# Expert numbers 21 to a register load, table sums three blocks at once, and a written order for SP in a mixture-of-experts stage

## The chip, the cores and the metric

The kernel runs on one core of a Trainium2 chip. A core has five engines that run side by side, each with its own instruction stream: TensorE (PE in the profile; PEld is its weight load), VectorE (DVE), ScalarE (ACT), GpSimd (POOL) and SyncE (SP, which mostly starts DMAs). They wait for each other through semaphores. The metric is device time in microseconds (us) of one launch; smaller is better. For several launches the median is given.

## The reference

An image of 2 x 256 channels x 56 x 56 goes through a convolution-like layer (group means and a ReLU), then through a transformer layer over N = 3136 tokens of 256 numbers for each of the two images: causal attention with four heads, and then a top-2 mixture of eight experts. The last part is what the change touches:

```python
t = t + _L1_attn_ref(_ln_t(t), L1_attn_W_attn, L1_attn_W_proj)
t = t + _L1_ffn_ref(_ln_t(t), L1_ffn_gate_w, L1_ffn_gate_b, ...)
...
probs = jax.nn.softmax(xf @ gate_w + gate_b, axis=-1)
top2_vals, top2_idx = jax.lax.top_k(probs, 2)
cw = jnp.zeros((N, Ee)).at[jnp.arange(N)[:, None], top2_idx].add(top2_vals)
for each expert e:
    out += cw[:, e] * (gelu(xf @ w1[e] + b1[e]) @ w2[e] + b2[e])
```

The loop over the experts is a scan in the reference; it is shortened here. Width 256, hidden width 512, all in 32-bit floats.

## The kernel before, in words

The kernel computes only the two experts that each token picks, so 2 x 2 x 3136 rows in all. It sorts these rows by expert into slots of a table in DRAM, in blocks of 128 slots that belong to one expert each: NBLK = 105 blocks.

**Dispatch.** `dispatch(b)` runs once for each of the two images, b = 0 and 1: softmax of the gate, top two, a rank for every picked row (matmuls into `rank` and `total`), the slot of each row, the expert of each block (`eblks[b]`), the biases of the blocks (matmuls into `bp`). Then POOL scatters the rows, two indirect DMAs from each of NCH = 25 tiles `xr`, to the table `xds[b]` (L1108). The tiles of image 1 come from a pool `sx` of 10 buffers. The first FULL0 = 42 blocks hold rows of image 0 alone. The blocks up to MIXED = 57 may hold rows of both images, and these are in two tables: a block's input there is the sum of its rows of both.

**Experts.** `experts` (L1124) is the stage from about 895 to 1352 us. Its loop runs n from -1 to 107 and does in iteration n, in written order:

- `fetch(g)`: starts the DMA of a group of GB = 3 blocks from the table to a tile `xb` (three buffers), six blocks ahead; for groups 14 to 18 also that of the other table to `xo` (one buffer).
- `load(g)`: two blocks ahead; for image 1 the tokens to which results go (`to`), and a register load (L1162) of the three experts of the group, one on PE and one on DVE, because both address weights by the expert's number.
- `hidden(n)`: eight matmuls into `ht` (L1202) and four Gelu on ACT to `g` (L1211).
- `inputs(n + 1)`: for blocks 42 to 56 adds the block's `xo` rows to its `xb` rows on DVE (L1176); two transposes on PE into `tp` (L1179) and a copy on ACT to `xT` (L1183).
- `weights(n + 2)`: DVE copies the expert's first weights to `w` (L1190), at an address taken from a register.
- `outputs(n - 3)`: four matmuls into `yp` (L1220) with the expert's second weights in `w2s`, also addressed by a register; DVE adds the bias to give `ys` (L1228); blocks below 57 are stored by SP to `y_slots`, blocks from 42 on are scattered by POOL to `y_tokens` (L1234).
- `between()`: pulls two pieces of other work (three while image 1's rows are being scattered) from a queue of generators.

**The queue of other work.** `pull` (L1359) takes the first generator that has something to do. `yield True` ends a piece of work, `yield False` says that nothing can be done yet. In the queue are `closing` (the end of attention, then `judge`), `tokens` with the rest of `dispatch(1)`, and from block 57 on `finish(0)`, which gathers image 0's results from `y_slots` and writes them out. `finish(1)` runs after the loop. `judge` (L1343) looks at the largest and the smallest row sum of the softmax and counts, with a matmul into `gdp`, whether all lie within bounds; the number `good` is read by all engines at the end, where the program branches on it.

**Attention's end.** The last block of attention is scaled while the expert stage begins: `sum_rows` (a matmul into `sp` L681, a copy to `line` L686, DMAs), `invert` (reciprocals, DMAs to `inverses` and `rb`), `scale` (L713), then the projection into `pp` (L563).

**What sets the order.** Inside `tc.manual_schedule(engines={PE, DVE, POOL})` these three engines run their instructions in the order in which the program is written. ACT and SP are ordered by a scheduler: SP's DMA starts may stand earlier or later in its stream than they are written. A tile waits for a free buffer of its pool before it is written, and a queue that reaches such a wait holds everything behind it.

Of the kernel before, what the change touches and what calls it, by code (L numbers as in the profile page):

```python
# [16 lines left out]
PE = mybir.EngineType.PE  # L17
DVE = mybir.EngineType.DVE
POOL = mybir.EngineType.Pool

MASKED = -1.0e30
LOWEST = -3.0e38
# [3 lines left out]
def conv_attn_moe_kernel(  # L26
# [71 lines left out]
    MIXED = MOST0 + E  # L98
    NBLK = (2 * B * N + E * (P - 1)) // P
    GB = 3  # L100
    SCALE = 1.0 / HS**0.5
    LEAST, MOST = 1e-25, 1e25
    assert B == 2 and NBLK % GB == 0 and FULL0 % GB == 0 and QB % (2 * P) == 0
    assert E % HEADS == 0 and NCH * XW <= NH * E * H

    def chunk(j):
# [318 lines left out]
    def layer1(nm, general):  # L425

        with ExitStack() as whole:
# [471 lines left out]
            def dispatch(b):  # L899
# [59 lines left out]
                flat = both.rearrange("p t e -> p (t e)")  # L959
                yield from small_piece()  # L960


                rank = bank(f"rank_{b}")
                nc.tensor.matmul(rank[:, : NCH * E], keep01, flat, start=True, stop=True)
# [118 lines left out]
                hot = g1.tile([E, w], F32, tag="hot", name=f"hot_{nm}{b}")  # L1083
                nc.vector.tensor_tensor(hot, eb[:E, :w], row.to_broadcast([E, w]), ALU.is_equal)
                yield from small_piece()
                bp = bank(f"bp_{b}", (P, KH, w))
                for k in range(KH):
                    nc.tensor.matmul(bp[:, k, :], b1s[:, k, :], hot, start=True, stop=True)
# [35 lines left out]
            def experts(w1s, w2s, b2s, ex, es, ps6, between, need, written):  # L1124
# [25 lines left out]
                def load(g, xb, other):  # L1150
                    s, e = g * GB, (g + 1) * GB
                    b = 0 if e <= FULL0 else 1
                    to = None
                    if b:

                        eq = es.tile([P, GB], F32, tag="eq", name=f"eq_{nm}_{g}")
                        nc.vector.tensor_tensor(eq, xb[:, :, C + 1], slot_id[:, s:e], ALU.is_equal)
                        nc.vector.tensor_scalar(eq, eq, -float(N), float(N + OFF), ALU.mult, ALU.add)
                        to = ex.tile([P, GB], U32, tag="to", bufs=4, name=f"to_{nm}_{g}")
                        nc.vector.tensor_tensor(to, eq, xb[:, :, C], ALU.add)  # L1160
                    f = known[b][0]
                    _, eids = nc.values_load_multi_w_load_instructions(  # L1162
                        eblks[b][0:1, s - f : e - f],
                        engines=(PE, DVE),
                        min_val=0,
                        max_val=E - 1,
                        skip_runtime_bounds_check_because="a count of at most E parts, cut to E - 1",
                    )
                    return xb, other, to, eids

                def inputs(n, group):
                    xb, other, to, eids = group
                    g = n % GB
                    rows = xb[g] if n < GB else xb[:, g, :C]
                    if FULL0 <= n < MIXED:
                        nc.vector.tensor_tensor(rows, rows, other[:, g, :C], ALU.add)  # L1176
                    tp = ps6.tile([P, 512], F32, tag="tp", bufs=2, name=f"tp_{nm}_{n}")
                    for c in range(NH):
                        nc.tensor.transpose(  # L1179
                            tp[:, c * P : (c + 1) * P], rows[:, c * P : (c + 1) * P], ident  # L1180
                        )
                    xT = es.tile([P, NH, P], F32, tag="xT", name=f"xT_{nm}_{n}")
                    nc.scalar.copy(xT.rearrange("p c t -> p (c t)"), tp[:, : NH * P])  # L1183
                    return xT, to, eids[g]

                def weights(n, group):

                    w = es.tile([P, NH, H], F32, tag="w", bufs=2, name=f"w_{nm}_{n}")
                    e = group[3][n % GB]
                    nc.vector.tensor_copy(  # L1190
                        w, w1s[:, :, bass.ds(e, 1), :].rearrange("p c e h -> p c (e h)")
                    )
                    return w

                def hidden(n, state, w):
                    xT, to, e = state
                    ht = ps6.tile([P, KH, P], F32, tag="ht", bufs=2, name=f"ht_{nm}_{n}")
                    g = es.tile([P, KH, P], F32, tag="g", bufs=LATE + 2, name=f"g_{nm}_{n}")
                    b = int(n >= FULL0)
                    for k in range(KH):  # L1200
                        for c in range(NH):
                            nc.tensor.matmul(  # L1202
                                ht[:, k, :],
                                w[:, c, k * P : (k + 1) * P],
                                xT[:, c, :],
                                start=(c == 0),
                                stop=(c == NH - 1),
                            )
                    for k in range(KH):
                        i = n - known[b][0]  # L1210
                        nc.scalar.activation(  # L1211
                            g[:, k, :], ht[:, k, :], AF.Gelu, bias=b1bs[b][:, k, i : i + 1]
                        )
                    return g, to, e

                def outputs(n, state):
                    g, to, e = state
                    yp = ps6.tile([P, 512], F32, tag="yp", bufs=2, name=f"yp_{nm}_{n}")
                    for k in range(KH):
                        nc.tensor.matmul(  # L1220
# [26 lines left out]
                    if n == MIXED - 1:  # L1247
                        written()

                fetched, groups, xin, wb, act = [], [], {}, {}, {}  # L1250
                for n in range(-1, NBLK + LATE):
                    while len(fetched) * GB <= min(n + 6, NBLK - 1):
                        fetched.append(fetch(len(fetched)))
                    while len(groups) * GB <= min(n + 2, NBLK - 1):
                        groups.append(load(len(groups), *fetched[len(groups)]))
                    if 0 <= n < NBLK:
                        act[n] = hidden(n, xin.pop(n), wb.pop(n))
                    if n + 1 < NBLK:
                        xin[n + 1] = inputs(n + 1, groups[(n + 1) // GB])
                    for m in (n + 1, n + 2):  # L1260
                        if m < NBLK and m // GB < len(groups) and m not in wb:
                            wb[m] = weights(m, groups[m // GB])
                    if 0 <= n - LATE < NBLK:
                        outputs(n - LATE, act.pop(n - LATE))
                    between()
# [77 lines left out]
            def judge():  # L1343

                tiles = g1.tile([P, 4], F32, tag="judge", name=f"judge_{nm}")
                flat_sums = sums.rearrange("p r f -> p (r f)")
                nc.vector.tensor_reduce(tiles[:, 0:1], flat_sums, AX.X, ALU.max)
                nc.vector.tensor_reduce(tiles[:, 1:2], flat_sums, AX.X, ALU.min)
                nc.vector.tensor_scalar(tiles[:, 2:3], tiles[:, 0:1], MOST, None, ALU.is_le)
                nc.vector.tensor_scalar(tiles[:, 3:4], tiles[:, 1:2], LEAST, None, ALU.is_ge)  # L1350
                nc.vector.tensor_tensor(tiles[:, 2:3], tiles[:, 2:3], tiles[:, 3:4], ALU.mult)
                gdp = bank("gdp")
                nc.tensor.matmul(gdp[:1, :1], tiles[:, 2:3], ones[:, 0:1], start=True, stop=True)
                nc.vector.tensor_copy(good, gdp[:1, :1])
# [51 lines left out]

            att = whole.enter_context(ExitStack())
            end = whole.enter_context(ExitStack())
            px = pool(att, "px", bufs=2)
            aw = pool(att, "aw", bufs=1)  # L1410
            kT = aw.tile([P, NH, N], F32, name=f"kT_{nm}")
# [12 lines left out]
            else:  # L1424
# [18 lines left out]
                    while at[b] + 1 < PARTS * (s + 1) and step(b):  # L1443
                        pass

                att.enter_context(tc.manual_schedule(engines={PE, DVE, POOL}))
                for b in range(B):
                    queue.append(tokens(b, qT, lambda b=b: min(finished[b])))

# [23 lines left out]
            def closing():  # L1473

                if not general:
                    while finished[B - 1][NH - 1] < N:
                        clock[0] += 4
                        due(clock[0])
                        yield True
                        yield True  # L1480
                    while not projected[B - 1]:
                        yield False
                    judge()
                end.close()
                scatter_rows.append(pool(whole, "sx", bufs=10, side="right"))
                yield True

            queue.appendleft(closing())
            with ExitStack() as moe:
# [17 lines left out]
                        pull()  # L1507

                def written():
                    oy = pool(moe, "oy", bufs=2, side="right")  # L1510
                    queue.append(finish(0, oy, 2))

                with tc.manual_schedule(engines={PE, DVE, POOL}):
                    experts(
                        first[0], w2s, b2s, ex, es, ps6,
                        lambda: pull(3 if ranked[1] and not sent[1] else 2), need, written,
                    )
# [74 lines left out]
```

## Time and profile before

| | us |
|---|---|
| median of 4 launches | 1396.59 |
| lowest, highest | 1393.25, 1399.71 |
| the profiled launch, its own time | 1399.56 |
| span of the profiled launch | 1397.5 |
| attention and conv layer before the expert stage | 0 to about 895 |
| expert stage | about 895 to 1353 |
| tail (`finish(1)`) | 1353 to 1397.5 |

The page gives busy time of each engine, a table of the span in 40 slices, and the chain of work that ended last, followed back from the last instruction. A group line reads: line of the kernel, engine, operation, output<-input by the program's names, count, busy time and mean length. TENSOR_LOAD is a load of registers; it is run by an engine's sequencer, which the page writes as PEldq, DVEq. "Idle before" is time in which the engine had nothing to run, with the instruction that ended it; "issue" is a wait that the profile does not explain, and "another core or an unknown queue" a semaphore whose setter is not found.

By stage (columns: us, PE busy, PEld busy, DVE busy, ACT busy, POOL busy with instruction counts, the granted share of PE's full clock, busy share of the DMA engines, GB/s):

```profile
410.00:895.00 485.00, 474.90 (x4536) 209.14 (x4528) 336.45 (x547) 256.82 (x355) 91.66 (x71) 1.00 0.11 34
895.00:1353.00 458.00, 420.37 (x2827) 386.97 (x2828) 189.54 (x477) 162.95 (x547) 173.41 (x170) 0.97 0.38 119
1353.00:1397.50 44.50, 15.52 (x55) 9.12 (x53) 21.54 (x51) 7.30 (x13) 1.92 (x2) 0.54 0.69 219
```

How to read it: in the tail PE is busy 15.52 of 44.5 us and the DMA engines 0.69 of it; in the expert stage PE is busy 420.37 of 458.

### The profile page before, as it was taken

Reading aid. Unit: us, or ns where it says so; the run is one execution under the profiler, and the core shown is the slowest. Engines: PE = TensorE matmul, PEld = TensorE weight load, DVE = VectorE, ACT = ScalarE, POOL = GpSimd, SP = SyncE. Lnnn points to the kernel's source line nnn. Section 1 sums busy time; section 2 is a strip of 40 time slices with the busy share of each in tenths; the row PEclk is TensorE's granted clock in tenths of the full one; section 3 lists DMA queues with packets and bytes.
Section 4 is the critical chain, followed back from the end, with each engine's and each line's share of the span. In section 5 each row is a group of like instructions: output and inputs, shape, how many; then the busy total and the mean of one; then the engine's idle time right before and its main releaser. Section 6 shows DMA issues by size and latency. Waiting matters only on the chain.

```text
span 1397.5 us, 27499 instructions
## 1 busy us (share of the span) xinstructions
PE 1305.7 (93%) x10642; PEld 822.9 (59%) x10642; DVE 780.4 (56%) x1525; ACT 610.4 (44%) x1197; POOL 311.3 (22%) x299
## 2 busy tenths in 40 slices
PE   8998999999999999999999999879889998999973
PEld 7864444444444444444444444469789988999872
DVE  1562555757777455677577887547333333444435
ACT  0244554545565554654445565533223333343322
POOL 1102111010000111110333430000562024555530
PEclk9999999999999999999999999999999999999995
DMA  9992000000000001000011123442433233444427
GB/s 299 382 310 88 23 15 25 28 12 20 16 9 23 8 1 37 16 9 16 31 42 43 54 71 119 132 138 63 139 125 96 91 103 100 129 140 138 127 83 246
DMA packets 107889, 123.89 MB, mean 89 GB/s; under 512 B 18863, under 2 KB 97340, under 8 KB 107624
## 3 DMA queue, kind: packets, MB, share of 16 engines
q1 hardware_dynamic: 89976, 89.67, 20.8%
q0 software_dynamic: 10416, 26.00, 5.6%
q10 hardware_dynamic: 7360, 6.39, 1.4%
q8 instruction: 87, 1.43, 0.5%
q14 instruction: 50, 0.41, 0.1%
HBM read 63.04 MB, written 60.81 MB: 89 GB/s over the span
## 4 chain that ended last, share of the span: by engine, by line
PE 73%; issue 9%; DMA 3%; ACT 2%; another core or an unknown queue 1%; DVE 1%; POOL 1%; DVEq 0%; POOLq 0%; ACTq 0%; SPq 0%
PE yp_f L654 17%; PE sc_f L614 17%; PE ht_f L1202 12%; PE yp_f L1220 12%; PE qk_f L513 5%; PE pp_f L563 3%; PE v_f L527 3%; DMA out_dram<-ot_f 2%; PE tp_f L1179 2%; ACT g_f L1211 1%; PE sp_f L681 1%; ACT st_f L622 1%; POOL xn_f L482 1%; PE xp_f L500 1%
## 5 line engine op out<-in xcount | busy, mean ns | idle before, releaser
L636 DVE TENSOR_TENSOR acc_f<-acc_f,st_f 128x896 f32<-128x896 f32 (+5 forms) x372 | 366.7, 986 | 167.9 <-ACT st_f L622 158.0
L622 ACT ACTIVATE st_f<-sc_f 128x896 f32<-128x896 f32 (+5 forms) x400 | 333.8, 838 | 285.8 <-PE sc_f L614 254.6
L654 PE MATMUL yp_f<-st_f,v_f 64*64 64x448 f32 (+6 forms) x3184 | 341.7, 505 | 7.1 <-DVE qT_f L665 5.7
L614 PE MATMUL sc_f<-qT_f,kT_f 64*64 64x448 f32 (+6 forms) x3184 | 342.2, 501 | 0.7 <-ACT st_f L622 0.7
L1202 PE MATMUL ht_f<-xT_f,w_f 128*128 128x128 f32 x1680 | 213.5, 282 | 31.0 <-ACT xT_f L1183 13.8
L1211 ACT ACTIVATE g_f<-ht_f,b1b 128x128 f32<-128x128 f32 x420 | 120.1, 368 | 277.3 <-PE ht_f L1202 175.9
L1202 PEld LDWEIGHTS ht_f<-xT_f,w_f 128*128 128x128 f32 x1680 | 207.5, 197 | 42.1 <-ACT xT_f L1183 18.4
L614 PEld LDWEIGHTS sc_f<-qT_f,kT_f 64*64 64x64 f32 x3184 | 117.2, 133 | 153.0 <-issue 137.7
L654 PEld LDWEIGHTS yp_f<-st_f,v_f 64*64 64x64 f32 x3184 | 111.7, 133 | 157.5 <-issue 132.0
L1220 PE MATMUL yp_f<-w2s_f,g_f 128*128 x840 | 199.6, 381 | 0.0
L482 POOL TENSOR_SCALAR xn_f<-t 128x256 f32<-128x256 f32 (+1 forms) x50 | 68.9, 1388 | 543.5 <-issue 324.2
L1108 POOL DMA_INDIRECT x_slots<-xr_f,idx x100 | 114.0, 1140 | 246.3 <-DVE xr_f L1100 144.6
L1220 PEld LDWEIGHTS yp_f<-w2s_f,g_f 128*128 128x128 f32 x840 | 152.9, 192 | 16.9
L1190 DVE COPY w_f<-w1s_f 128x1024 f32 x105 | 74.3, 708 | 106.3 <-PE ht_f L1202 55.2
L1228 DVE TENSOR_TENSOR ys_f<-yp_f,b2s_f 128x256 f32<-128x256 f32 x105 | 44.5, 424 | 130.4 <-PE yp_f L1220 100.5
L513 PE MATMUL qk_f<-xT_f,wat 128*128 128x512 f32 (+1 forms) x224 | 97.7, 580 | 4.2 <-ACT xT_f L506 4.2
L1234 POOL DMA_INDIRECT y_tokens<-ys_f,to_f x63 | 63.5, 1008 | 160.5 <-DVE ys_f L1228 85.1
L624 DVE TENSOR_TENSOR st_f<-st_f,keep 128x256 f32<-128x256 f32 (+1 forms) x112 | 43.5, 388 | 83.9 <-ACT st_f L622 67.8
L513 PEld LDWEIGHTS qk_f<-xT_f,wat 128*128 128x128 f32 x224 | 40.1, 197 | 59.1 <-issue 46.6
L1291 POOL DMA_INDIRECT y_f<-y_slots,idx x50 | 55.3, 1106 | 16.2 <-issue 15.0
L563 PE MATMUL pp_f<-wpr,qT_f 128*128 128x264 f32 (+1 forms) x200 | 53.6, 403 | 0.6 <-DVE qT_f L713 0.6
L527 PE MATMUL v_f<-wv,xT_f 128*128 128x264 f32 (+1 forms) x200 | 50.9, 398 | 0.0
(210 smaller groups left out, 884.4 us busy)
## 6 DMA issues: line engine op xcount, KB each, us to landing
x_slots<-fill SPq DMA_DIRECT2D x1, 8127.0 KB
xb_f<-x_slots SPq DMA_DIRECT2D x21, 387.0 KB
x_slots<-fill SPq DMA_DIRECT2D x1, 7296.0 KB
y_slots<-ys_f SPq DMA_DIRECT2D x57, 128.0 KB
kept<-t SPq DMA_DIRECT2D x2, 3200.0 KB
x<-in_x_dram SPq DMA_DIRECT2D x14, 448.0 KB
xr<-in_x_rows_dram SPq DMA_DIRECT2D x12, 512.0 KB
y_f<-y_tokens SPq DMA_DIRECT2D x24, 256.0 KB
```

The costliest lines, as they stand in the source:

```text
L482: nc.gpsimd.tensor_scalar(xn[:k, a], ts[b][:k, n + a, :C], ts[b][:k, n + a, MEAN : MEAN + 1], ts[b][:k, n + a, RSTD : RSTD + 1], ALU.subtr ...
L513: nc.tensor.matmul(ps[:, :w], wat[:, c, d0 : d0 + P], xT[:, c, :w], start=(c == 0), stop=(c == NH - 1),)
L527: nc.tensor.matmul(ps[:k, : C + E], xT[:, c, o : o + k], wv[:, c].rearrange("p h d -> p (h d)"), start=(c == 0), stop=(c == NH - 1),)
L563: nc.tensor.matmul(ps[:k, : C + E], qT[:, c, o : o + k], wpr[:, c, :], start=(c == 0), stop=(c == NH - 1),)
L614: nc.tensor.matmul(ps[h : h + HS, a, c0:W], kT[rows, hp, j * P + h : j * P + h + HS], qT[rows, hp, q0 + c0 : q0 + W], start=True, stop=True,)
L622: nc.scalar.activation(st[:k, :, c0:], ps[:k, :, c0:W], AF.Exp, scale=SCALE)
L636: nc.vector.tensor_tensor(acc[:k, :, c0:], acc[:k, :, c0:], st[:k, :, c0:], ALU.add)
L654: nc.tensor.matmul(yp[a * HS : (a + 1) * HS, h // HS, c0:W], v[h : h + HS, j, 2 * hp + a, :HS], st[h : h + HS, a, c0:], start=first, stop= ...
L1108: s = nc.gpsimd.indirect_dma_start(out=xds[b], out_offset=bass.IndirectOffsetOnAxis(ap=idxs[b][:kk, k, n : n + 1], axis=0), in_=xr[:kk], i ...
L1202: nc.tensor.matmul(ht[:, k, :], w[:, c, k * P : (k + 1) * P], xT[:, c, :], start=(c == 0), stop=(c == NH - 1),)
L1211: nc.scalar.activation(g[:, k, :], ht[:, k, :], AF.Gelu, bias=b1bs[b][:, k, i : i + 1])
L1220: nc.tensor.matmul(yp[:, :C], g[:, k, :], w2s[:, k, bass.ds(e, 1), :].rearrange("p e d -> p (e d)"), start=(k == 0), stop=(k == KH - 1),)
```

## The change

The diff has six parts.

1. Registers: a load now takes RB = 21 experts at once, so each of PE and DVE issues five loads instead of 35, in iterations -1, 19, 40, 61 and 82, each with 21 registers. `load` no longer does it; `experts_of(r)` does, right after `load` in the iteration.
2. Adds: the sum of both tables' rows is made in `load`, one instruction of up to three blocks, instead of one for each block in `inputs`. There are five instead of 15; each comes an iteration before the block's transposes.
3. SP joins the engines of the written order, in both places.
4. The pool `sx` has 25 buffers instead of 10; it is opened in a context of its own and closed in `written`, before `finish(0)`'s pool is made.
5. `judge` is a generator in three pieces: the reductions; the three small operations; and, one empty pull later, the matmul with its copy.
6. `dispatch(1)` has two more `yield True`, ahead of `rank` and ahead of `bp`.

In the engines' streams: POOL's order stays the same; `gdp` stands one block later in PE's; image 1's first scatter comes in iteration 18 instead of 15 and its last in 34 instead of 31; SP's DMA of the first `xo` and three of `finish(0)`'s residual loads (`res`) stand later than before, the other `xo` starts earlier, each right after its `xb` (before, each stood three `y_slots` stores later); on ACT the pair of table loads around image 1's Exp stands one block later.

```diff
+SP = mybir.EngineType.SP
...
     GB = 3
+    RB = 21
...
                 flat = both.rearrange("p t e -> p (t e)")
                 yield from small_piece()
 
+                if b:
+                    yield True
 
                 rank = bank(f"rank_{b}")
...
                 yield from small_piece()
+                if b:
+                    yield True
                 bp = bank(f"bp_{b}", (P, KH, w))
...
-                    f = known[b][0]
-                    _, eids = nc.values_load_multi_w_load_instructions(
-                        eblks[b][0:1, s - f : e - f],
+                    if other is not None:
+                        mixed = min(e, MIXED) - s
+                        nc.vector.tensor_tensor(
+                            xb[:, :mixed, :C], xb[:, :mixed, :C], other[:, :mixed], ALU.add
+                        )
+                    return xb, to
+
+                def experts_of(r):
+
+                    b = 0 if (r + 1) * RB <= FULL0 else 1
+                    s = r * RB - known[b][0]
+                    return nc.values_load_multi_w_load_instructions(
+                        eblks[b][0:1, s : s + RB],
                         engines=(PE, DVE),
...
-                    if FULL0 <= n < MIXED:
-                        nc.vector.tensor_tensor(rows, rows, other[:, g, :C], ALU.add)
...
                     while len(groups) * GB <= min(n + 2, NBLK - 1):
                         groups.append(load(len(groups), *fetched[len(groups)]))
+                    if len(ids) <= min(n + 2, NBLK - 1):
+                        ids.extend(experts_of(len(ids) // RB))
...
                 nc.vector.tensor_reduce(tiles[:, 1:2], flat_sums, AX.X, ALU.min)
+                yield True
                 nc.vector.tensor_scalar(tiles[:, 2:3], tiles[:, 0:1], MOST, None, ALU.is_le)
...
+                yield True
+                yield True
                 gdp = bank("gdp")
...
-                att.enter_context(tc.manual_schedule(engines={PE, DVE, POOL}))
+                att.enter_context(tc.manual_schedule(engines={PE, DVE, POOL, SP}))
...
-                    judge()
+                    yield from judge()
                 end.close()
-                scatter_rows.append(pool(whole, "sx", bufs=10, side="right"))
+                scatter_rows.append(pool(spread_rows, "sx", bufs=NCH, side="right"))
...
                 def written():
+                    spread_rows.close()
...
-                with tc.manual_schedule(engines={PE, DVE, POOL}):
+                with tc.manual_schedule(engines={PE, DVE, POOL, SP}):
```

More of the change, by code (lines that the diff above doesn't have):

```diff
@@ L100, in conv_attn_moe_kernel @@
     GB = 3
+    RB = 21
     SCALE = 1.0 / HS**0.5
     LEAST, MOST = 1e-25, 1e25
-    assert B == 2 and NBLK % GB == 0 and FULL0 % GB == 0 and QB % (2 * P) == 0
+    assert B == 2 and NBLK % GB == 0 and FULL0 % RB == NBLK % RB == FULL0 % GB == 0 and QB % (2 * P) == 0
     assert E % HEADS == 0 and NCH * XW <= NH * E * H
@@ L1167, in load @@
                         skip_runtime_bounds_check_because="a count of at most E parts, cut to E - 1",
-                    )
-                    return xb, other, to, eids
+                    )[1]
                 def inputs(n, group):
-                    xb, other, to, eids = group
+                    xb, to = group
                     g = n % GB
                     rows = xb[g] if n < GB else xb[:, g, :C]
-                    if FULL0 <= n < MIXED:
-                        nc.vector.tensor_tensor(rows, rows, other[:, g, :C], ALU.add)
                     tp = ps6.tile([P, 512], F32, tag="tp", bufs=2, name=f"tp_{nm}_{n}")
@@ L1183, in inputs, with weights @@
                     nc.scalar.copy(xT.rearrange("p c t -> p (c t)"), tp[:, : NH * P])
-                    return xT, to, eids[g]
-                def weights(n, group):
+                    return xT, to
+                def weights(n):
                     w = es.tile([P, NH, H], F32, tag="w", bufs=2, name=f"w_{nm}_{n}")
-                    e = group[3][n % GB]
+                    e = ids[n]
                     nc.vector.tensor_copy(
@@ L1195, in hidden @@
                 def hidden(n, state, w):
-                    xT, to, e = state
+                    xT, to = state
                     ht = ps6.tile([P, KH, P], F32, tag="ht", bufs=2, name=f"ht_{nm}_{n}")
@@ L1213, in hidden @@
                         )
-                    return g, to, e
+                    return g, to
                 def outputs(n, state):
-                    g, to, e = state
+                    g, to = state
+                    e = ids[n]
                     yp = ps6.tile([P, 512], F32, tag="yp", bufs=2, name=f"yp_{nm}_{n}")
@@ L1248, in outputs @@
                         written()
-                fetched, groups, xin, wb, act = [], [], {}, {}, {}
+                fetched, groups, ids, xin, wb, act = [], [], [], {}, {}, {}
                 for n in range(-1, NBLK + LATE):
@@ L1260, in experts @@
                     for m in (n + 1, n + 2):
-                        if m < NBLK and m // GB < len(groups) and m not in wb:
-                            wb[m] = weights(m, groups[m // GB])
+                        if m < NBLK and m not in wb:
+                            wb[m] = weights(m)
                     if 0 <= n - LATE < NBLK:
@@ L1408, in layer1 @@
             end = whole.enter_context(ExitStack())
+            spread_rows = whole.enter_context(ExitStack())
             px = pool(att, "px", bufs=2)
```

## The prediction

> **What bounds the kernel now.** I read the page first: busy times, then the chain of work that ended last.
>
> ```profile
> span 1397.5 us, 27499 instructions
> ...
> PE 1305.7 (93%) x10642; PEld 822.9 (59%) x10642; DVE 780.4 (56%) x1525; ACT 610.4 (44%) x1197; POOL 311.3 (22%) x299
> ...
> PE 73%; issue 9%; DMA 3%; ACT 2%; another core or an unknown queue 1%; DVE 1%; POOL 1%; DVEq 0%; POOLq 0%; ACTq 0%; SPq 0%
> ```
>
> TensorE (PE) sets the end, and nothing in the diff removes a matmul. So only PE's idle time can be won: 91.8 us of the span, plus blocks run at a low clock. The change touches the expert stage (895 to 1352 us). I next read the chain there, piece by piece.
>
> ```profile
> 936.53 0.26 DVE judge_f L1347
> ...
> 987.74 1.73 PE yp_f L1220 x8
> 989.47 1.41 issue
> 990.88 2.05 PE ht_f L1202 x16
> ...
> 998.11 7.53 another core or an unknown queue
> 1005.66 1.15 ACT g_f L1211 x4
> 1006.81 0.76 issue
> 1007.56 3.79 PE ht_f L1202 x16
> ...
> 1033.58 3.51 issue
> 1037.09 3.78 PE ht_f L1202 x16
> ```
>
> Columns: start, length, what. A steady block is 1.78 (ht, 8 matmuls with their weight loads) + 0.22 (transposes) + 1.73 (yp) = 3.73 us. Two pieces here are not work (7.53 and 3.51), and the ht after each takes 3.79 and 3.78, twice 1.78: in the window 999 to 1011 the granted clock is 0.76. Third, the operations that the diff edits:
>
> ```profile
> L1162 DVEq TENSOR_LOAD <-eblk x35: 740/877/1005, 895.0 to 1329.8; - x35
> L1162 PEldq TENSOR_LOAD <-eblk x35: 763/782/1412, 895.0 to 1326.0; - x35
> ```
>
> ```profile
> L1176 DVE TENSOR_TENSOR xb_f<-xb_f,xo_f x15: 415/425/426, 1086.5 to 1145.2; 128x256 f32<-128x256 f32 x15
> ...
>   PE tp_f L1179: 2.9, 5
> ```
>
> The first shows 35 loads of three registers, 0.78 us (PE) and 0.88 us (DVE). The second shows 15 adds, for which PE waited five times.
>
> Against 3.73 us a block, blocks 0 to 103 lose 58.4 us. The timeline puts it at: blocks 2 and 3 9.2 (start chain, w2s), 4 and 5 3.0, judge (6 and 7) 3.0, rank and bp matmuls 1.8, five load blocks at 975 to 1060 us and the blocks behind them 18.0, adds 5.6, blocks 62, 63, 67, 81, 88, 91 and 95, in or just behind later load blocks, 14.0, yo transposes the rest.
>
> **The verdict in pieces.** Before, the reductions (two of 0.26), three small operations and gdp stand in one piece; PE, in written order, waits at gdp 936.07 to 937.50 = 1.43 for DVE, then 0.64 for the next ht and 0.22 at 942.30: 2.3, and block 7 adds about 0.2. After, gdp stands a block later, 3.73 us for work of about 1.4. Value -2.5 (0 to -3). Should dispatch(0)'s work, which moves along in the same queue, cover DVE instead, 1.4 comes back.
>
> **Adds for three blocks at once.** Fifteen adds of 0.425 become five of 128x3x256, moved from the block's transposes to load(), a block earlier. PE waits 0.58 to 0.59 at tp for five of the adds (from 1095.37, 1107.35, 1119.32, 1131.43 and 1145.17 on), and from 1136.08 on 1.44 for an add whose xo came late. By blocks: 43, 46, 49 0.78 each, 52 0.92, 53 1.63, 55 0.77 = 5.66. The new add is not in the trace: between 0.425 (if its length counted least) and 3 x 0.425 = 1.28; I take 1.28, the elements being threefold. DVE is 56% busy over the span and the add has a block of lead, 3.73, so it is hidden: -5.6 (0 to -5.7). Uncovered it would cost five times 1.28 = 6.4.
>
> **SP in written order.** SP is now in manual order: xo stands right behind its xb, three y_slots stores no longer ahead of it, two early hoists (first xo, three res) gone. xo has one buffer, so SP waits at xo(g) for add(g-1), at most a block; queued behind it are y_slots stores of ys, with three buffers, 3 x 3.73 = 11.2 us of slack. res is wanted by finish(0) some blocks on. POOL's queue keeps its order; on ACT only the pair of table loads round dispatch(1)'s Exp (1.28 each) moves, by one block. Cost 0; if the slack were gone, a block each at five groups at most, 18.7.
>
> **A scatter buffer per tile; two yields in dispatch(1).** Buffers 10 to 25. DVE's waits before xr ended at once in before; POOL waits for DVE (144.6 us at L1108), not for buffers. So 0 for the buffers. The yields put dispatch(1)'s scatters two to three blocks later (first xr at iteration 18 instead of 15, last at 34 instead of 31); rank and bp matmuls get a block more to wait, 1.0 at most of the 1.8 above. The last group that needs them is fetched at iteration 36, so cover is two blocks, 7.5 us; gone, it would be paid at once. Value 0 (-1 to +4).
>
> **Registers: 21 at a time.** Thirty-five loads become five on each engine, at iterations -1, 19, 40, 61, 82. No row has a 21-register load. Single-register loads (`good`, 0.31 PE, 0.55 DVE) and three-register ones (0.78, about 0.75 at DVE's shortest) give a slope per register of (0.78 - 0.31)/2 = 0.235 on PE and 0.10 on DVE: 21 registers 0.78 + 18 x 0.235 = 5.0 or 0.75 + 18 x 0.10 = 2.6. Flat, it would be 0.8. I take 4.0, between the two slopes and nearer PE's own row. A load stands 2.8 us ahead of PE's next need (load 1014.47, ht 1017.3; 1026.86, 1029.7), which hides 0.78 wholly (load blocks at 3.73) but leaves 4.0 - 2.8 = 1.2 per load: four in the stream, +4.8 (0 to 4 x 2.2 = 8.8). DVE has about 5 us of slack before w(n+2): 0; gone, 4 each.
>
> The skill's page "Runtime: NRT & Kernel Launch", section "Instruction fetch mechanics", says a register load costs about 200 ns per register even in bulk, a rule against this change: by it 21 cost about 4.2 us, an estimate, and the sum would have 5.6 in place of 4.8. The rows of one and three registers above (0.31, 0.78) agree within 20% on PE; on DVE they give half of it.
>
> At the start the first load (895.01, 0.96) stands in PE's order ahead of the row-sum matmul whose copy (line_f, 897.69) begins the chain of DMAs to inverses (911.72 + 4.16) and pp (920.63). A load of 4.0 delays it by up to 3.0, partly covered because w2s lands no sooner than 914: +2 (0 to 4).
>
> **Late semaphores.** The 7.53 and 3.51 above: PE's last ht or yp ends, but its semaphore arrives 1.2 to 5.5 us later, so ACT's g_f and DVE's w_f start together at 1005.66. In 975 to 1060, while POOL scatters 50 times, this happens in load blocks only: gaps of PE at 989.47, 1002.34, 1021.19, 1033.58, 1051.30, each 6.7 us behind a load (982.76, 995.63, 1014.47, 1026.86, 1044.59). Five of five; no other block. Load blocks without dense POOL transfers (1057 to 1141) show none. If the loads cause it, after has one in that window (iteration 19) in place of five: 18.0 less the 1.6 of block 19. I count -16.4 here, and 0 for the later ones (those from 67 on hold 7.2, but loads at 61 and 82 remain, and the gaps there stand less regularly behind loads), and +2 because the remaining one may be longer.
>
> Sum: 1399.56 - 2.5 - 5.6 + 4.8 + 2 - 16.4 + 2 = 1383.9. The profiled execution took 1399.56, its span 1397.5 with 2.06 around it, and is 2.97 above the median 1396.59; the same subtracted gives 1380.9: **1381**.
>
> **Rivals.**
> (B) Late semaphores come from POOL's transfers, not from loads. For: they also appear at 1174 to 1313 during gathers, with less regularity; and loads recur each third block, so a chance phase is possible. Against: five of five. Sum without -16.4 + 2: 1399.56 - 1.3 - 2.97 = 1395.3.
> (C) Slower: stalls grow with the load's length. For: what is late may wait for the load's own reads, and 4.0 is 5.1 times 0.78. Before, some 11 load blocks in POOL's windows cost 18 + 14 = 32, or 2.9 each; after, three (19, 61, 82) at 2.9 x 5.1 = 14.8 cost 44.4. That is +12.4 with the rest at -1.3: 1396.59 + 11.1 = 1407.7. It decides from 33.3/3 = 11.1 us a load. Against: records show loads no longer than 1.4 in those windows.
> (D) The change doesn't reach PE: SP's written order makes an xb or xo late, and the adds move ahead of their data; the 5.6 remains and 18.7 is a ceiling: 1381 + 5.6 + 9 = 1396. For: xo has one buffer. Against: 11.2 us of slack.
>
> **How the numbers follow.** My forecast 0.48, B 0.20, C 0.24, D 0.08. A measurement of this kernel can't tell a change under 0.5% (7 us) from none. Faster than 1389.6: forecast 0.46, B 0.05, C 0 and D 0.01 = 0.52; slower than 1403.6: C 0.20, D 0.02, B 0.01 = 0.23; same 0.25. The forecast's own range is 1372 to 1390: later stalls gone too (-9), or loads at 8.8 and start at 4 (+6) and the judge or adds gaining less (+3). For 8 in 10 it runs from 1371 to 1405, leaving out half of C and the ends of the forecast.
>
> **What would show it.** Right: five TENSOR_LOADs per engine of 2.6 to 5.0 us; gaps only near iteration 19 in the scatter window and no half clock at 1007 and 1037; no PE wait at gdp or tp for the adds; line_f at about 899.7. B is shown by the same gaps at blocks without loads; C by a gap over 11 us after a load; D by PE waiting for an xb transfer. I am wrong if a load takes much over 5 us, or if the gaps leave without the loads.

## The result, and the profile after

The changed kernel takes 1401.11 us (median of 42 launches), the kernel before 1397.99 (63 launches on the same chips). The ratio is 1.0022 (95% interval 1.0013 to 1.0031): 3.1 us slower, where 15.7 us faster were forecast; with so many launches a difference of 0.22% can be told from none, less than half of the 0.5% that the prediction allowed for. The profiled launch of the changed kernel took 1407.04, above all its timed launches (1394.21 to 1405.07), so single waits of it are checked below against other runs that share its parts.

The changed kernel's page, busy times and chain:

```profile
span 1404.9 us, 27419 instructions
...
PE 1310.7 (93%) x10642; PEld 827.8 (59%) x10642; DVE 778.9 (55%) x1515; ACT 610.5 (43%) x1197; POOL 313.0 (22%) x299
...
PE 75%; issue 9%; DMA 3%; ACT 3%; POOL 1%; DVE 1%; another core or an unknown queue 1%; ACTq 0%; DVEq 0%; POOLq 0%; SPq 0%
```

PE is busy 5.0 us longer with the same matmuls, so more of them ran at a low clock (the mean granted clock is 0.969, before 0.972). The loads and adds that the change edits (group, engine, operation, count: shortest/median/longest ns, first and last start):

```profile
L1178 DVEq TENSOR_LOAD <-eblk x5: 1600/4849/5548, 893.3 to 1257.7; - x5
L1178 PEldq TENSOR_LOAD <-eblk x5: 1831/5167/6077, 893.4 to 1254.4; - x5
```

```profile
L1169 DVE TENSOR_TENSOR xb_f<-xb_f,xo_f x5: 945/947/958, 1089.8 to 1134.6; 128x768 f32<-128x768 f32 x5
```

The adds take 0.95 us, not 1.28, and no one is listed as waiting for them. The loads have no middle: on PE two take 1.83 and 1.87, three 5.17, 5.59 and 6.08. What each group of blocks loses against 3.73 us a block, worked out from the starts of `ht` in each profile (us; the columns are the kernel before, the changed kernel and five of the experiments below):

| blocks | before | changed | E1 | E5 | E6 | E7 | E9 |
|---|---|---|---|---|---|---|---|
| 0-5 start | 11.8 | 9.9 | 10.7 | 11.7 | 9.8 | 12.3 | 11.3 |
| 6-17 verdict, dispatch | 5.0 | 7.5 | 7.5 | 6.1 | 5.0 | 2.2 | 7.4 |
| 18-36 scatters | 18.3 | 25.3 | 21.7 | 18.5 | 21.6 | 15.1 | 20.6 |
| 43-56 sums of two tables | 5.8 | 0.0 | 0.0 | 0.0 | 0.0 | 0.0 | 0.0 |
| 57-79 | 10.1 | 10.3 | 13.1 | 6.5 | 10.5 | 2.5 | 10.6 |
| 80-84 | 2.1 | 8.2 | 2.4 | 2.0 | 7.0 | 0.9 | 2.4 |
| 85-103 | 6.0 | 6.4 | 9.9 | 6.0 | 6.0 | 2.9 | 6.0 |

The 5.8 us of the adds is won in every kernel that has them. It is given back in three places: 6-17 (+2.5), 18-36 (+7.0 in this profile) and 80-84 (+6.1). The columns add up to 59.1 and 67.6: this one launch loses 8.5 us more, the medians differ by 3.1.

The changed kernel has one load in the scatter window, at 982.4 on PE, where in the kernel before five loads each stood ahead of a gap. The chain of work that ended last still has the two long gaps (start, length, what):

```profile
1011.64 3.56 issue
1015.20 3.78 PE ht_f L1215 x16
...
1041.85 3.53 issue
1045.38 3.40 PE ht_f L1215 x16
```

They stand 29 and 59 us behind that load, and the next load comes at 1086.0.

### The profile page after: what moved, and what is told of

Its sections match the earlier page's. It is cut to its first block, busy times and chain, and to the rows that moved or that the text cites. A ratio compares the mean times of both kernels' runs of the same rounds, so it can differ in the third digit from the quotient of the medians.

```text
span 1404.9 us, 27419 instructions
## 1 busy us (share of the span) xinstructions
PE 1310.7 (93%) x10642; PEld 827.8 (59%) x10642; DVE 778.9 (55%) x1515; ACT 610.5 (43%) x1197; POOL 313.0 (22%) x299
## 4 chain that ended last, share of the span: by engine, by line
PE 75%; issue 9%; DMA 3%; ACT 3%; POOL 1%; DVE 1%; another core or an unknown queue 1%; ACTq 0%; DVEq 0%; POOLq 0%; SPq 0%
PE yp_f L656 17%; PE sc_f L616 17%; PE ht_f L1215 14%; PE yp_f L1234 12%; PE qk_f L515 5%; PE pp_f L565 3%; PE v_f L529 3%; PE tp_f L1192 2%; DMA out_dram<-ot_f 2%; ACT g_f L1224 1%; ACT st_f L624 1%; PE sp_f L683 1%; POOL xn_f L484 1%; PE xp_f L502 1%
## 5 line engine op out<-in xcount | busy, mean ns | idle before, releaser
L1215 PE MATMUL ht_f<-xT_f,w_f 128*128 128x128 f32 x1680 | 217.4, 285 | 39.6 <-issue 18.5
```

Source lines behind the costliest of these rows:

```text
L1215: nc.tensor.matmul(ht[:, k, :], w[:, c, k * P : (k + 1) * P], xT[:, c, :], start=(c == 0), stop=(c == NH - 1),)
```

## The experiments

Ratios are to the kernel before on the same chip; "changed" is the changed kernel's 1.0022.

**E1: three experts to a load.**

```diff
-    RB = 21
+    RB = 3
```

> The changed kernel with three experts to a register load again (35 loads instead of 5); all else as changed. Theory 1: the 21-register loads take 5 to 6 us while POOL's indirect DMAs run (5.17, 5.59, 6.08 in the profile; 1.8 in the two quiet places) and hold PE at blocks 18, 61 and 82, where the changed kernel lost 2.7 + 4.7 + 7.0 us. Without them the time falls by 5 to 10 us against the changed kernel, to 0.993 to 0.998 of the kernel before. Theory 2 (loads are innocent, the losses there are the late semaphores that come with dense POOL traffic): ratio stays at 1.000 to 1.004, and stalls of the same size appear beside blocks 61 and 82.

Measured: 0.999 (0.9974 to 1.0006), 0.32% or 4.5 us faster than changed, just under the 5 to 10 of theory 1. Blocks 80-84 fall from 8.2 to 2.4, and block 18 loses nothing. Blocks 60 and 61 lose 0.3 instead of 4.7, but blocks 62 and 63 now lose 7.3 instead of 0.8, at the place where the kernel before lost 6.7. The stalls of blocks 21 to 36 stay, at the same blocks 21, 24, 27, 30 and 33, with a three-register load every third block as with one long load in the whole window. So the long loads cost time, and the stalls of the scatter window are something else.

**E2: without the two yields in dispatch(1).**

```diff
-                if b:
-                    yield True
```

(in both places)

> The changed kernel without the two extra yields in image 1's dispatch. Theory 1: the loss of 4.6 us at blocks 9 and 10 (PE waits 2.65 behind the Exp of ACT L930 and its table loads) comes from where those yields and the split verdict put the Exp, not from the yields alone, so it stays, and the scatter window only moves back by three blocks: 0 to -3 us against the changed kernel. Rival: the yields are the loss; then blocks 9 and 10 go back to 0.7 us and the time falls by 4 to 7 us. In both, stalls in the scatter window stand every ninth scatter, whatever block that is.

Measured: 1.0036 (1.0014 to 1.0058), not told apart from changed. Blocks 9 and 10 keep 2.8 and 1.8 us, so the rival falls. Theory 1 had that place right, but not the time, nor the way in which the scatters move: blocks 11 and 16 now lose 1.9 and 2.7 at the `rank` and `bp` matmuls, against 0.7 and 1.1 (at blocks 12 and 17), and the first scatter comes only 1.5 us earlier (985.1 against 986.6), not three blocks. The yields give cover for DVE, worth 2.8 us in the profile; what moved the scatters was the verdict (E6).

**E3: SP ordered by the scheduler.**

```diff
-engines={PE, DVE, POOL, SP}
+engines={PE, DVE, POOL}
```

> The changed kernel with SP ordered by the scheduler again. Theory 1: SP's order is worth nothing: ratio within 0.3% of the changed kernel, stalls of the scatter window still every ninth scatter. Rival: SP's written order starts the table's DMA (xb) within 1 to 3 us before each stall of the scatter window in the changed kernel, and causes the stalls; then their sum (25 us over blocks 18 to 35) falls by more than half and the time by 10 us or more.

Measured: 1.0007 (0.999 to 1.0023), not told apart from changed (the intervals overlap); blocks 18 to 36 lose 20.7, with the stalls at the same scatters. SP's order is not the cause.

**E4: a slower pace of scatters.**

```diff
+                def paced():
+                    turn[0] += 1
+                    pull((3 if turn[0] % 2 else 2) if ranked[1] and not sent[1] else 2)
...
-                        lambda: pull(3 if ranked[1] and not sent[1] else 2), need, written,
+                        paced, need, written,
```

(on E2's kernel)

> The changed kernel without the two yields, and with three and two pieces in turn (instead of always three) pulled in a block while image 1 is scattered, so that POOL starts 2.5 scatters a block of 3.73 us (3.2 us at 1.28 each) instead of 3 (3.84 us). Theory 1: the late semaphores come from POOL running scatters without a pause for nine or more in a row; with a pause in each two blocks they are gone or under 1 us: the scatter window loses under 6 us instead of 25, and the time falls by 12 us or more against the run without the yields alone. Rival (the stalls follow the table's DMA or a load in each third block): stalls stay at every third block and the window loses 18 to 25 us.

Measured: 0.9986 (0.9965 to 1.0007), 0.5% faster than E2, yet blocks 18 to 36 still lose 15.2: both theories missed. What it did show is the rhythm. Which scatter of image 1 is the next to start when PE begins to wait, read off the timelines:

```
               scatters a block   scatter number            blocks
before         3                  10, 18, 28, 36, 46        19, 22, 25, 28, 31
changed        3                  8, 16, 26, 34, 44, 47     21, 24, 27, 30, 33, 34
E1             3                  8, 16, 26, 34, 44         21, 24, 27, 30, 33
E4             2.5                10, 20, 28, 40, 50        21, 25, 28, 33, 37
```

At three scatters a block a stall at about each ninth scatter falls on each third block. At 2.5 it leaves the three-block grid and stays at 8 to 12 scatters. It follows POOL's DMAs, not the blocks. One rival is left: DVE's copies to `xr` go at the same pace as the scatters, and no run slowed one without the other. E2, with pauses in POOL's work, is less regular (14, 20, 27, 31, 38, 46).

**E5: the adds alone, on the kernel before.**

```diff
+                    if other is not None:
+                        mixed = min(e, MIXED) - s
+                        nc.vector.tensor_tensor(
+                            xb[:, :mixed, :C], xb[:, :mixed, :C], other[:, :mixed], ALU.add
+                        )
...
-                    if FULL0 <= n < MIXED:
-                        nc.vector.tensor_tensor(rows, rows, other[:, g, :C], ALU.add)
```

> The kernel before with one part of the change: the adds of both tables' rows as one instruction for three blocks in load. Theory 1: blocks 43 to 56 lose nothing instead of 5.8 us, as in every profile that has these adds so far, and nothing else moves: 0.994 to 0.998 of the kernel before. Rival: the gain is hidden, because what sets the end lies elsewhere later (POOL's gathers, the transfers); then 0.999 to 1.001 with the loss of blocks 57 to 103 grown by as much.

Measured: 0.9947 (0.992 to 0.9973), as theory 1 had it: 7.4 us (3.8 to 11.2) of gain that is not hidden. The blocks of the adds explain 5.8 of it; in this profile block 62 also loses 1.3 instead of 5.0, which no part of the edit touches.

**E6: the verdict in one piece.**

```diff
-                yield True
...
-                yield True
-                yield True
                 gdp = bank("gdp")
...
-                    yield from judge()
+                    judge()
```

> The changed kernel with the verdict in one piece again. Theory 1: splitting it takes 2.0 us out of blocks 6 and 7 but lets image 1's Exp, with its table loads, fall where nothing covers it (blocks 9 and 10 lose 4.6 us in all profiles with the split); in one piece blocks 6 to 10 lose some 3.5 us together instead of 5.6, and the scatters start two to three blocks earlier: 0 to 4 us faster than the changed kernel. Rival: the two extra pieces of work in dispatch(1) move the Exp, not the verdict; then blocks 9 and 10 keep their 4.6 us and blocks 6 and 7 lose 2.0 us more: about 2 us slower than the changed kernel.

Measured: 0.998 (0.996 to 1.0001), 0.42% faster than changed; theory 1. Blocks 6 to 17 lose 5.0 as before the change, and the scatters start at 975.1. The timelines of ACT show why; first the kernel before, then the changed one (start, length, what, idle before):

```profile
936.04 0.39 ACT L1183 COPY xT_f<-tp_f 128x256 f32<-128x256 f32 x1
936.44 1.28 ACT L928 ACT_TABLE_LOAD   x1
939.38 0.37 ACT L928 ACTIVATE lg_f<-lg_f 128x200 f32<-128x200 f32 x1 [1.65 <-DVE lg_f L927]
939.77 1.28 ACT L1211 ACT_TABLE_LOAD   x1
```

```profile
943.44 0.37 ACT L1224 ACTIVATE g_f<-ht_f,b1b 128x128 f32<-128x128 f32 x1 [2.33 <-PE ht_f L1215]
943.83 1.28 ACT L930 ACT_TABLE_LOAD   x1
945.12 0.37 ACT L930 ACTIVATE lg_f<-lg_f 128x200 f32<-128x200 f32 x1
945.51 1.28 ACT L1224 ACT_TABLE_LOAD   x1
946.80 0.89 ACT L1224 ACTIVATE g_f<-ht_f,b1b 128x128 f32<-128x128 f32 x3
```

Before, Exp's first table load lies in the time in which PE waits for the verdict anyway. Changed, both loads and the Exp (2.97 us) stand between the first and the other three Gelus of one block. The next block's xT copy is behind them, and PE waits 2.65 us. That is the 2.8 of block 9. The 1.8 of block 10 is a low clock after the wait, and not all profiles with the split verdict have it, as the expectation says: in E3 block 10 loses 0.1.

**E7: transposes and weight copies a block further ahead.**

```diff
-    RB = 21
+    RB = 3
...
-                    if n + 1 < NBLK:
-                        xin[n + 1] = inputs(n + 1, groups[(n + 1) // GB])
-                    for m in (n + 1, n + 2):
+                    for m in (n + 1, n + 2):
+                        if m < NBLK and m not in seen_in:
+                            seen_in.add(m)
+                            xin[m] = inputs(m, groups[m // GB])
+                    for m in (n + 1, n + 2, n + 3):
```

(`w` three buffers instead of two, `g` four instead of five, groups and registers loaded one iteration earlier)

> The changed kernel with three experts to a load, and with the transposes and the copies of the first weights made one block further ahead (third buffer for w, four for g). Theory 1: the stalls of the scatter and gather windows are PE waiting for xT and w, which start late because PE's own semaphores arrive 1 to 6 us late about every ninth of POOL's indirect DMAs; one block (3.7 us) more of slack absorbs all stalls up to that: of the 21.7 us in blocks 18 to 36 under 8 remain, of 8.0 in 57 to 66 under 4, and the time falls by 15 us or more against three experts to a load (ratio 0.985 to 0.990 of the kernel before). Rival: PE itself is held (the stalls are PE's own, and its semaphores only show it): the stalls stay where they are, and the time within 3 us.

Measured: 0.9824 (0.9789 to 0.9858), 1374.39 us, 1.7% faster than E1. What ended PE's idle time before `ht`, first in E1, then here (us, times):

```profile
  ACT xT_f L1196: 54.2, 33
  issue: 29.3, 19
```

```profile
  issue: 5.8, 11
  ACT xT_f L1196: 1.4, 2
```

PE's waits for xT, 54.2 us, are 1.4. Blocks 57-79 lose 2.5 instead of 13.1. Of the 21.7 in the scatter window 15.1 remain, in three places (blocks 26, 30, 34), where PE pauses 0.5 to 1.0 us several times within a block, at 1007.39 (0.94) and 1008.95 (0.82) in the midst of `ht`'s matmuls; theory 1 left under 8. So it holds for the later blocks, and for part of the scatter window: there PE itself is held too, and the rival has a share.

**E8: loads moved away from POOL's DMAs.**

```diff
-                    if len(ids) <= min(n + 2, NBLK - 1):
+                    if len(ids) <= min(n + 2, NBLK - 1) or n in (14, 56):
```

> The changed kernel with the second 21-register load at iteration 14 and the fourth at 56, ahead of POOL's dense scatters and gathers, in place of 19 and 61. Theory 1: a 21-register load takes about 1.85 us without and 5 to 6 us with dense POOL DMAs: both fall below 2.5 us and are hidden, and blocks 18 (2.7) and 60 and 61 (4.7) lose under 1 us each unless a late semaphore falls there; the time falls by 3 to 6 us against the changed kernel. Rival: the length goes with the position in the table or the stage, not with POOL: the loads keep 5 us and blocks 14 and 56 lose 2.5 us each.

Measured: 1.0052 (1.003 to 1.0073), no faster than changed; blocks 13, 14 and 55 now lose 2.6, 1.7 and 2.8. The load at 960.4 took 5.16 us, and the window around it reads (span, PE, PEld, DVE, ACT, POOL busy, clock, DMA share, GB/s):

```profile
960.40:965.70 5.30, 2.95 (x19) 2.39 (x18) 3.93 (x16) 1.40 (x5) 0.00 (x0) 1.00 0.13 43
```

POOL did nothing. My theory that POOL's traffic makes the load long falls; the rival, the position in the table, holds. The first and third loads, at the start of a table, are the short ones.

**E9: the numbers of each load at a multiple of 128 bytes.**

```diff
-                nc.vector.tensor_copy(eblks[b], eb[:, :w])
+                for r, o in enumerate(AT[b]):
+                    nc.vector.tensor_copy(eblks[b][:, o : o + RB], eb[:, r * RB : (r + 1) * RB])
...
-                    s = r * RB - known[b][0]
+                    s = AT[b][r - known[b][0] // RB]
```

with `AT = ((0, 32), (0, 32, 64))`

> The changed kernel with the expert numbers of each 21-register load at an address that is a multiple of 128 bytes in the table (offsets 0, 32 and 64 elements) instead of 0, 21 and 42; two or three short copies on DVE write them. So far the loads at offset 0 (first and third) took 1.8 to 1.9 us in every run and those at 21 and 42 5.2 to 6.1, also where POOL was idle. Theory A: the address decides: all five take under 2.2 us, none holds PE, blocks 18, 60, 81 lose 2.7 + 2.9 + 4.0 us less, and the time falls by 5 to 10 us against the changed kernel (ratio 0.995 to 0.999). Theory B: the semaphore wait decides (the short ones are those that wait for DVE's write of the table, and their record starts later): the second, fourth and fifth keep 5 to 6 us and the time does not move.

Measured: 0.9964 (0.9948 to 0.998), 0.58% or 8.1 us faster than changed; theory A.

```profile
L1180 DVEq TENSOR_LOAD <-eblk x5: 1593/1596/1861, 892.4 to 1253.5; - x5
L1180 PEldq TENSOR_LOAD <-eblk x5: 1610/1779/2099, 892.4 to 1249.7; - x5
```

All ten loads are short. Blocks 80-84 lose 2.4 instead of 8.2, block 18 nothing. The fourth load saves nothing net: blocks 60 and 61 lose nothing instead of 4.7, but 62 and 63 lose 5.5 instead of 0.8, as in E1.

**E10: other offsets, one launch.** `AT = ((0, 24), (0, 22, 44))`

> As the aligned kernel, but with offsets 0 and 24 elements (96 bytes) in the first table and 0, 22 (88 bytes) and 44 (176 bytes) in the second. If the address decides, this shows the step: with a step of 8 bytes all are short (under 2.2 us), with 16 the fourth alone is long (5 us), with 32 the fourth and the fifth, with 64 or more the second too.

Measured (one launch, 1389.29 us): on PE 1.83, 1.63, 1.88, 5.52, 1.61; the fourth alone is long.

```profile
L1180 DVEq TENSOR_LOAD <-eblk x5: 1591/1848/4852, 892.5 to 1246.7; - x5
L1180 PEldq TENSOR_LOAD <-eblk x5: 1611/1828/5523, 892.5 to 1243.4; - x5
```

Short at 0, 96, 128, 176 and 256 bytes, long at 84, 88 and 168: of the offsets tried, multiples of 16 bytes are short and the others long. All ten of these loads wait for the same semaphore of DVE, so the wait (theory B) does not.

**E11 and E12: E7 with the verdict in one piece; then with 21 experts to a load at E9's offsets.** Their edits are those of E6 and E9.

> The kernel that prepares a block further ahead (three experts to a load), with the verdict in one piece. Theory 1: the two gains add: 0.9824 x (0.998 / 1.0022) = 0.978, some 1368 us. Rival: with the blocks prepared further ahead, the wait at the Exp's table load is absorbed already (blocks 9 and 10 lose nothing there with the split verdict), while in one piece the verdict holds PE for 2 us: 0.983 to 0.985.

> As the one before, with 21 experts to a load at addresses that are multiples of 128 bytes. If the address decides the length of a load, both kinds are hidden behind PE's 2.8 us of lead, and the ratio is within 0.3% of the one before. If it does not, three loads of 5 to 6 us cost 2.4 to 3.3 us each and it is 7 to 9 us slower.

Measured: 0.9822 (0.98 to 0.9844) and 0.9821 (0.98 to 0.9841), 1372.61 and 1373.84 us; neither is told apart from E7. The rival of E11 had the mechanism: with the further block the split verdict costs nothing (blocks 8 to 14 lose 0.8 in E7) and in one piece it holds PE (blocks 6 and 7: 1.9 against 0.3). With room to prepare ahead, short loads of 21 registers and loads of three cost the same; long loads of 21 were not tried there. All three beat both kernels by some 25 us.

## Why the prediction was wrong

**Late semaphores** is the step that failed. It gave the gaps of the scatter window to the register loads (-16.4 and +2) because five of five stood 6.7 us behind one. With one load in the window instead of five they stayed: blocks 18-36 lose 25.3 in the changed kernel (2.7 of it at block 18, right behind that load), 20.7 in E3, and 20.6 in E9, whose load is short, against 18.3 before. Where the step had 14.4 us less, E9 has 2.3 more and E10 0.7 less: some 14 to 17 of the 18.8 us between forecast and measurement. In the kernel before the loads came every third block, and so did every ninth scatter; its trace could not tell the two apart. The changed kernel's did, with gaps at blocks that have no load, the prediction's own sign for B, and E4 showed that they move with the pace of the scatters. So rival B pointed the right way, to POOL's transfers or to what keeps their pace. Its 1395.3 missed by 5.8: 1.4 of that is the base (1396.59 of four launches, 1397.99 of 63), and the loads and the verdict cost more than its sum held. That each stall goes with about nine of POOL's DMAs is a count, not a mechanism: why PE's semaphores come late there, or what holds PE, stays open.

**Registers, 21 at a time.** +4.8 (0 to 8.8) was right in kind, short in size: 8.1 us by E9 against changed. The price of 4.0, between two slopes, fits no load. The short loads make (1.83 - 0.31) / 20 = 0.08 a register, under the flatter slope of 0.10; the long ones, 5.17 to 6.08, make 0.24 to 0.29, at and over the steeper one of 0.235. Exposed were 2.4 to 3.3 us at three loads, not 1.2 at four, and a low clock behind two of them; the fourth load's share is no net loss, since blocks 62 and 63 lose as much without it. That a load takes over 5 us was also one of the prediction's own signs of being wrong.

The Trainium skill's page "Runtime: NRT & Kernel Launch", section "Instruction fetch mechanics", has about 200 ns a register, so 21 would take about 4.2 us, an estimate. This case shows 1.6 to 2.1 us at multiples of 16 bytes and 4.7 to 6.1 at the others, so here the measurement decides. The page calls its loads "uncached AXI"; these read a tile in SBUF.

**The start.** The +2 did not come. Blocks 0 to 5 lose 9.9 instead of 11.8: the load at 893.4 took 1.83, not 4.0, and line_f starts at 896.41, not at 899.7. Over all profiles the kernels with 21 registers to a load lose 9.3 to 11.4 there, those with three 10.7 to 12.3: a gain of about 1 us at best, which the spread does not settle.

**The verdict in pieces.** -2.5 was right for blocks 6 and 7 (3.0 to 1.0) and wrong as a sum: the wait that it removed covered Exp's table load, which then cost 2.8 us at block 9 and, by a low clock in most profiles with the split, 1.8 at block 10. The step named dispatch(0)'s work on DVE as what might come next; it was dispatch(1)'s on ACT, and "moves by one block" was costed at nothing.

**Adds.** -5.6, measured -5.8 in the blocks and 7.4 (3.8 to 11.2) alone. Price and place were right.

**SP's order, the yields.** 0 holds for SP within the intervals. The yields save about 2.8 us in the profile (E2) where I had 0 (-1 to +4), and they are not what put the scatters later: without them the first comes 1.5 us earlier, with the verdict in one piece 11.5 (E6). The 25 buffers were not tried alone.

Together, by ratios: -0.53% (adds) + 0.42% (verdict) + 0.58% (loads) = +0.47%, less the yields' 0.14% (E2, unsure) +0.33%, against 0.22% measured, which the intervals allow. SP's order (E3, +0.15%) is as unsure as the yields and would cancel them. The 58.4 us that the prediction counts as lost in blocks 0 to 103 are 59.1 by the table above; no term of its sum rests on the total.

## What to carry to other kernels

When a stall recurs with a period, count what else has that period before naming a cause: three blocks were one register load, and also nine scatters. Here, where PE waits for another engine's answer in every block, one more block of preparation won 23 us (E7 against E1), more than making any single wait shorter. Removing a wait exposes what lay under it; look at every engine's timeline there, not only at the one that waited.

## What the runs showed of the hardware

- A load of 21 registers took 1.6 to 2.1 us when its first address was a multiple of 16 bytes within the table (0, 96, 128, 176 and 256) and 4.7 to 6.1 when it was not (84, 88 and 168), on PE and DVE alike.
- In the scatter window PE's semaphores arrive 1.2 to 6.0 us after the recorded ends of its matmuls, at about every ninth indirect DMA of POOL. The profile models the ends of matmuls, so this does not tell a late semaphore from a PE that is held.
- The length of a pause did not settle whether PE's clock fell after it. The pause of 2.65 us at block 9 was followed by a clock of 0.69 and 0.72 in the changed kernel, and by 1.00 in E3 (948.4 to 954.0) and E8 (947.5 to 953.0). A pause of 2.39 us left it at 1.00, one of 2.10 in E2 was followed by 0.58 (1029.9 to 1034.0), one of 3.49 in E10 by 1.00 (1012.1 to 1016.0). The changed kernel after its pauses of 2.65 and 2.39 us (columns as in E8, 0.69, 0.72 and 1.00 being the clock):

```profile
948.00:951.40 3.40, 3.40 (x20) 3.31 (x21) 2.40 (x6) 0.70 (x3) 0.00 (x0) 0.69 0.12 39
951.40:953.70 2.30, 2.30 (x10) 1.93 (x9) 0.00 (x0) 0.71 (x3) 0.00 (x0) 0.72 0.00 0
...
987.80:991.50 3.70, 3.69 (x26) 3.52 (x27) 0.25 (x1) 1.41 (x5) 1.00 (x1) 1.00 0.20 71
```
